# A graph layer's sums over edges on one core: four loads under way, 21 blocks of output kept back, and half as many paired sums

## The chip, the cores and the metric

The kernel runs on one NeuronCore of a Trainium2 chip. The metric is the device time of one execution in microseconds; three timed runs of the kernel before gave a median of 301.53 us (299.49 to 303.27). All data are float32.

## The reference

There are 12,500 nodes with 128 features and 412,500 edges with 48 features, sorted by their receiving node `dst`.

```
agg = segment_sum(edge_attr_48, dst, 12500)
h   = relu(layernorm(x))
u   = graph_globals[0]                       # every node belongs to graph 0
hid = relu(concat([h, agg, u]) @ W1 + b1)    # 256 wide
out = x + hid @ W2 + b2
```

The layer norm has no scale or shift of its own. The source nodes of the edges are not used.

## The kernel before, in words

**The sums over edges.** The edges are cut into 58 steps of 8 chunks; a chunk is 128 partitions by 7 edges. One load (`load`, line 297; the DMA itself is line 144) fetches two chunks, 336 KB, so a step has four loads; the last step has two, and a tail. For each step, VectorE builds a table of ones and zeros (`onehot`, line 308, tile `oh`) that says to which of 32 neighbouring nodes an edge goes. TensorE multiplies that table with the edges' features (`aggregate`, line 334) and adds up in PSUM (tile `ps`): eight chunks by seven places give 56 products of 32x48. ScalarE copies the result to `sums` (`keep_sums`, line 355), and about two steps later TensorE moves it to the right node rows with a second table (`place`, line 378, tile `pp`); VectorE adds it to the table of all sums `aggT` in SBUF (`add`, line 386).

The list `LEVELS` has one number for each step, 0 to 14. So many of the step's 14 groups (seven places, two halves of four chunks) are summed "by twos": two chunks are taken in one product of 64x96, of which only the two diagonal quarters are used. A group is then two products in place of four, and `keep_sums` makes two extra small copies in a step that has any.

```
if t >= n - twos:
    for q in range(0, CH, 2):
        c = CH * h + q
        product(ps[W * q:W * (q + 2), h], oh[:, c // 2, t], both[s][c // 2][:, :, t * DE:(t + 1) * DE],
                start=first, stop=end, skip_group_check=True)
    continue
```

**The layer.** The nodes are 26 blocks: one of 212 rows, 23 of 512, two of 256. For each block the rows of `x` are loaded (`load_x`, line 393), normalised (VectorE and ScalarE), turned (`turn`, tile `pt`), multiplied with the first weights (`first_h`, tile `ph`), and once all sums of the block are in, with the weights of the sums (`first_a`, tile `ph`); ScalarE takes the relu (`relu`, tile `hid`), TensorE the second product (`second`, tile `po`), VectorE adds x and b2 (`result`, line 527), and `store` (line 536) issues the output's DMA from POOL's queue (the last two blocks from SP's).

**The order.** It is written out by hand: each engine runs its instructions in the order in which the loop over steps (line 854) records them. The work of the layer is spread over half steps (`todo`, `at`) by a planner with a share of time for each. During step s the loads of step s + 3 are issued from SP's queue, one at each of four places in the step.

**What limits the loads.** `few` (line 290) makes each load wait until the load `FLIGHT` places before it has landed, and until TensorE has come to that place of the step (`last`):

```
def few(now):
    if len(flight) == FLIGHT:
        tc.add_manual_dep(now.ins, flight.pop(0).ins.name, LANDED, reason="few loads under way")
    flight.append(now)
    if paced:
        tc.add_manual_dep(now.ins, last[0], LANDED, reason="in TensorE's pace")
```

Loads of edges, of x and of node indices count alike. There are 18 buffers for loads of edges, four and a half steps' worth.

**Rows kept back.** The blocks in `HELD` do not get a buffer for their result: `result` writes it over the block's own, no longer needed columns of `aggT`, and `store` issues it in the last three steps (from half step 110 on, line 812), where few loads are left. The other blocks are stored as soon as they are done.

Of the kernel before, what the change touches and what calls it, by code (L numbers as in the profile page):

```python
# [22 lines left out]
def kernel(  # L23
# [38 lines left out]
    NS = NSF + 1  # L62
# [33 lines left out]
    NBL = len(blocks)  # L96
# [3 lines left out]

    FIRST = (1, 2, 3, 0, 4)

    HELD = range(NBL - 4 - 16, NBL - 4)
    ZN = 16
    zw = -(-(N + WG) // ZN)

# [43 lines left out]
    def rows_of(ap, a, m, r):  # L150
        return ap[a:a + m * r].rearrange("(p r) d -> p (r d)", r=r)
# [6 lines left out]
    with fast:  # L158
# [131 lines left out]
# [6 lines that stand above are left out]
# [38 lines left out]
        def aggregate(s, h, twos):  # L334
            left = s == NSF and h
            if h == 0:
                banks_s[s] = ps_agg.tile([P, 512], F32, name="ps")[:, :4 * DE].rearrange("p (h f) -> p h f", h=2)
            ps, es, oh = banks_s[s], edges[s], onehots[s]
            n = TT if left else T
            for t in range(n):  # L340
                first, end = t == 0 and h == 0, t == n - 1
# [6 lines that stand above are left out]
                for q in range(1 if left else CH):  # L348
                    c = CH * h + q
                    o = DE * (q % 2) if twos else 0  # L350
                    product(
                        ps[W * q:W * (q + 1), h, o:o + DE], oh[:, c // 2, t, c % 2], es[c][:, t * DE:(t + 1) * DE],
                        start=first, stop=end, skip_group_check=True)
# [32 lines left out]
        def add(s):  # L386
            _, v = nc.values_load_multi_w_load_instructions(  # L387
                at_i[0:1, s:s + 1], engines=[DVE], min_val=low(s), max_val=high(s),
                skip_runtime_bounds_check_because="clamped to these on the chip")
            to = aggT[:HI + DE, ds(v[0], WG)]  # L390
            nc.vector.tensor_tensor(to, to, banks_p.pop(s)[:HI + DE, :WG], OP.add)  # L391
# [135 lines left out]
        def result(j):  # L527
            a, m, r = blocks[j]
            if j in HELD:
                ot = aggT[:, BEFORE + a:BEFORE + a + r * D].rearrange("p (r d) -> p r d", d=D)  # L530
# [5 lines left out]
        def store(j):  # L536
# [3 lines left out]
            for p0, p1 in by_rows(m):  # L540
                now = queue.dma_start(rows_of(out, a + p0 * r, p1 - p0, r), ov[p0:p1])  # L541
                if j in HELD:
                    tc.add_manual_dep(now.ins, last[0], LANDED, reason="edges first")
# [58 lines left out]

        AHEAD = 4
        EARLY = 2
        FLIGHT = 5


        LEVELS = (0, 0, 0, 0, 7, 0, 0, 9, 14, 3, 14, 14, 0, 14, 3, 3, 2, 0, 5, 14, 0, 14, 2, 3, 0, 4, 14, 0, 14, 2, 4, 0, 3, 0, 5, 14, 0, 14, 0, 4, 0, 2, 0, 3, 14, 0, 14, 4, 2, 2, 0, 2, 2, 4, 0, 0, 0, 0)
        LATE = NS - 7
        NEAR = len(FIRST) + 1  # L610
        with tc.manual_schedule():
# [82 lines left out]
            def at(k, f, *a):  # L694
                todo.setdefault(max(0, k), []).append((f, a))
# [48 lines left out]
            for i in range(1, len(FIRST)):  # L744
                k = 2 * i
# [38 lines left out]
            for j in range(NW):  # L784
# [8 lines left out]
                if j + 1 < NW:  # L793
                    hidden_x(j + 1)
                    at(where["o", j] + 1, result, j)
                    if j not in HELD:
                        at(where["o", j] + 1, store, j)
# [3 lines left out]
            for j in range(NBL):  # L801
                if j in FIRST:
                    continue
                k = where["turn", j]
# [5 lines left out]
                at(k - 2, normal, j)  # L810
            at(where["a", 0] - 2, bias_of_globals)
            for i, j in enumerate(HELD):
                k = 2 * (NS - 3) + i // 3
                assert where["o", j] + 1 < k
                at(k, store, j)

# [3 lines left out]
            def apart(k, f, *a):  # L820
                while k - 1 in taken or k in taken or k + 1 in taken:
                    k -= 1
                taken.add(k)
                at(k, f, *a)
                return k
# [3 lines left out]
            for i in range(2, len(parts)):  # L829
                need = 2 * (parts[i][0] // CS - (4 if i == len(parts) - 1 else 0))  # L830
                k = apart(need - 4, middles, i)
                at(k + 2, check_dst, i)
                k = apart(k - 1, spread_dst, i, 1)
                k = apart(k - 1, spread_dst, i, 0)
# [5 lines left out]
            k = apart(2 * (NS - 6), verdict)  # L840
# [13 lines left out]
            for s in range(NS):  # L854
# [27 lines left out]
                if s >= LATE:  # L882
                    for p in now:
                        place(p)
                        add(p)
                twos = [max(0, LEVELS[s] - T), min(T, LEVELS[s])]
                aggregate(s, 0, twos[0])
# [175 lines left out]
```

## Time and profile before

| | |
|---|---|
| median of three timed runs | 301.53 us (299.49 to 303.27) |
| profiled execution | 298.43 us, of which the span is 296.6 us |
| TensorE (PE) busy | 283.1 us, 95% of the span |
| VectorE (DVE) busy | 237.0 us, 80% |
| ScalarE (ACT) busy | 161.0 us, 54% |
| POOL busy | 73.7 us, 25% |
| moved by DMA | 95.19 MB, mean 321 GB/s |
| loads of edges | 230 of 336 KB, median 5.2 us from issue to landing |
| mean granted TensorE clock | 0.991 |

PE is the matmul part of TensorE and PEld its weight loads, which overlap it. In the trace each float32 product shows as two records, so 56 products are "x112". In a row of the waits, the figures are the sum in microseconds, how often, and the longest. In a row of DMA issues they are how many, the size of each, and the median from issue to landing. In a row of the timeline they are the start, the length, the engine, the line, the operation, what it writes and reads, and how many were merged. In a row by windows each engine has its busy time and, in brackets, how many instructions ended there; the last three figures are the granted clock, the DMA engines' share of busy time and the rate.

### The profile page before, as it was taken

The page shows a single profiled execution, that of the slowest core. Times are in us where ns is not written, and L with a number is a line of the kernel's source. Part 1 is how long each engine was busy: PE and PEld are TensorE (multiplying, and loading weights), DVE is VectorE, ACT ScalarE, POOL GpSimd, SP SyncE. Part 2 cuts the span into 40 slices and gives each one's busy share as a digit, 9 for nine tenths or more (in the row PEclk, how much of TensorE's full clock was granted, in tenths as well). Part 3 has the DMA queues.
Part 4 walks back from the last instruction along what each step waited for, and adds up shares of the span by engine and source line. Part 5 has one row for each costly group of instructions (what it writes and reads, how often), then busy time and mean ns, then how long its engine had stood idle before and what let it go on. Part 6 is the DMA issues. An engine that isn't in the chain of part 4 may idle for free.

```text
span 296.6 us, 15062 instructions
## 1 busy us (share of the span) xinstructions
PE 283.1 (95%) x6553; PEld 223.5 (75%) x6554; DVE 237.0 (80%) x537; ACT 161.0 (54%) x399; POOL 73.7 (25%) x88
## 2 busy tenths in 40 slices
PE   6799897999999999999999999999999999999992
PEld 2657666898878778878878788867877977787781
DVE  6838969699998997887978699698986799986222
ACT  3477557323756664743666458644651985664420
POOL 3032381130212563021022212021111022103720
PEclk9999998999999999999999999999999999999998
DMA  6999999999999999999999999999999999999962
GB/s 162 372 314 345 272 358 313 370 370 370 356 357 356 326 367 285 298 348 290 332 312 339 346 345 317 336 321 322 310 347 337 353 298 323 337 352 317 363 222 81
DMA packets 69815, 95.19 MB, mean 321 GB/s; under 512 B 5018, under 2 KB 64739, under 8 KB 69743
## 3 DMA queue, kind: packets, MB, share of 16 engines
q1 hardware_dynamic: 67583, 87.66, 89.1%
q0 software_dynamic: 2160, 6.50, 6.1%
q8 instruction: 53, 0.87, 1.2%
q14 instruction: 19, 0.16, 0.1%
HBM read 87.74 MB, written 6.40 MB: 317 GB/s over the span
## 4 chain that ended last, share of the span: by engine, by line
PE 81%; DVE 8%; ACT 3%; DMA 2%; issue 2%; SPq 1%; DVEq 1%
PE ps L195 30%; PE ph L195 21%; PE po L195 14%; PE pp L195 10%; PE pt L199 5%; DVE oh L312 3%; DMA e<-in_edge_attr_dram 2%; DVE place L374 2%; ACT xn L438 1%; ACT hT L452 1%; PE pt L195 1%; DVE st L408 1%; DVE aggT L391 1%; DVE ph L489 1%; DVEq L387 1%
## 5 line engine op out<-in xcount | busy, mean ns | idle before, releaser
L312 DVE TENSOR_TENSOR oh<-iota,rel 128x1792 f32<-128x1792 f32 (+1 forms) x60 | 120.5, 2009 | 0.4 <-ACT rel L270 0.4
L195 PEld LDWEIGHTS ps<-e,oh 128*32 128x32 f32 (+1 forms) x5448 | 94.7, 116 | 21.7 <-issue 5.8
L195 PE MATMUL ps<-e,oh 128*32 128x48 f32 (+1 forms) x5448 | 106.5, 217 | 3.1 <-issue 1.2
L360 ACT COPY sums<-ps 128x192 f32<-128x192 f32 (+2 forms) x129 | 36.7, 285 | 78.7 <-PE ps L195 76.8
L431 POOL TENSOR_TENSOR xb<-xt,b_sb 128x512 f32<-128x512 f32 (+1 forms) x21 | 34.2, 1630 | 131.7 <-DVE aggT L533 79.4
L195 PE MATMUL ph<-hT,w1h 128*128 128x512 f32 (+2 forms) x100 | 49.6, 602 | 0.1
L195 PE MATMUL po<-w,hid 128*128 128x128 f32 (+1 forms) x376 | 48.0, 281 | 0.9 <-ACT hid L516 0.9
L516 ACT ACTIVATE hid<-ph,bias 128x512 f32<-128x512 f32 (+2 forms) x49 | 30.4, 670 | 30.4 <-PE ph L195 22.9
L195 PEld LDWEIGHTS po<-w,hid 128*128 128x128 f32 (+1 forms) x376 | 45.1, 196 | 2.0 <-ACT hid L516 1.3
L391 DVE TENSOR_TENSOR aggT<-aggT,pp 112x246 f32 x58 | 23.6, 406 | 24.5 <-PE pp L195 18.2
L195 PE MATMUL pp<-place,sums 128*112 128x128 f32 x232 | 39.0, 291 | 0.2 <-DVE place L374 0.2
L195 PEld LDWEIGHTS pp<-place,sums 128*112 128x112 f32 x232 | 28.9, 176 | 7.1 <-issue 1.7
L438 ACT ACTIVATE xn<-xt,sh,sc 128x128 f32<-128x128 f32 x80 | 33.1, 483 | 0.3
L374 DVE TENSOR_TENSOR place<-iota,pos 128x256 f32<-128x256 f32 x58 | 32.9, 569 | 0.0
L195 PE MATMUL ph<-aggT,w1a 48*128 48x256 f32 (+1 forms) x192 | 28.6, 402 | 0.2 <-DVE aggT L391 0.2
L195 PEld LDWEIGHTS ph<-aggT,w1a 48*128 48x128 f32 x192 | 17.2, 186 | 10.1 <-issue 6.8
L452 ACT COPY hT<-pt 128x512 f32<-128x512 f32 (+1 forms) x22 | 23.0, 1044 | 3.2 <-PE pt L199 3.1
L195 PEld LDWEIGHTS ph<-hT,w1h 128*128 128x128 f32 x100 | 16.7, 196 | 7.1 <-issue 4.6
L533 DVE TENSOR_TENSOR aggT<-po,xb 128x512 f32<-128x512 f32 x16 | 11.0, 685 | 9.2 <-PE po L195 9.2
L541 POOL DMA_DIRECT2D out_dram<-ot x9 | 5.0, 553 | 51.6 <-DVE ot L533 43.7
L408 DVE BATCH_NORM_STATS2 st<-xt 128x6 f32<-128x128 f32 x80 | 17.3, 277 | 0.0
L199 PE MATMUL pt<-ident,xn 128*128 128x128 f32 x84 | 14.1, 289 | 0.0
(137 smaller groups left out, 188.1 us busy)
## 6 DMA issues: line engine op xcount, KB each, us to landing
e<-in_edge_attr_dram SPq DMA_DIRECT2D x230, 336.0 KB, 5.2
xt<-in_x_dram SPq DMA_DIRECT2D x19, 256.0 KB, 4.9
out_dram<-aggT POOLq DMA_DIRECT2D x16, 256.0 KB, 4.5
out_dram<-ot POOLq DMA_DIRECT2D x7, 256.0 KB, 4.8
di<-in_dst_dram SPq DMA_DIRECT2D x3, 448.0 KB, 5.3
aggT<-in_x_dram SPq DMA_DIRECT2D x4, 256.0 KB, 4.2
xt<-in_x_dram SPq DMA_DIRECT2D x2, 128.0 KB, 4.6
out_dram<-ot SPq DMA_DIRECT2D x2, 128.0 KB, 3.3
```

What stands on the lines that cost most here:

```text
L195: last[:] = [nc.tensor.matmul(*a, **k).ins.name]
L199: last[:] = [nc.tensor.transpose(*a, **k).ins.name]
L312: nc.vector.tensor_tensor(to, iota[:, None, :W].to_broadcast([P, n, W]), r[:, :, None].to_broadcast([P, n, W]), OP.is_equal)
L360: nc.scalar.copy(to[k, h], ps[k, h, None, o:o + DE].to_broadcast([k.stop - k.start, h.stop - h.start, 2, DE]))
L374: nc.vector.tensor_tensor(po, iota[:, None, :WP].to_broadcast([P, 2, WP]), pos[:, s, :, None].to_broadcast([P, 2, WP]), OP.is_equal)
L391: nc.vector.tensor_tensor(to, to, banks_p.pop(s)[:HI + DE, :WG], OP.add)
L408: nc.vector.bn_stats(st[:m, q, :], xs[j][:m, q, :])
L431: nc.gpsimd.tensor_tensor(xb[:m, :r], xs[j][:m, :r], b2_sb[:m, None, :].to_broadcast([m, r, D]), OP.add)
L438: nc.scalar.activation(xn[:m, q], xs[j][:m, q], AF.Relu, bias=shift[j][:m, q:q + 1], scale=scale[j][:m, q:q + 1])
L452: nc.scalar.copy(hT[:, :m * r].rearrange("d (p r) -> d r p", r=r), ht[j][:, :m * r].rearrange("d (r p) -> d r p", r=r))
L516: nc.scalar.activation(to, ph, AF.Relu, bias=bias[:, h:h + 1])
L533: nc.vector.tensor_tensor(ot[:m, :r], pos_o[j][:m, :r], xbs[j][:m, :r], OP.add)
```

## The change

`FLIGHT` goes from 5 to 4: a load waits for the one four places before it. `HELD` takes blocks 1 to 21 in place of 6 to 21, so 21 results are kept in `aggT` and stored in the last three steps, four to a half step in place of three. `LEVELS` is another list: its sum is 121 in place of 248, and 29 of its entries are not zero in place of 35. Up to step 29 the sums are 63 and 155, up to step 50 they are 115 and 240.

```diff
-    HELD = range(NBL - 4 - 16, NBL - 4)
+    HELD = range(1, NBL - 4)
...
-        FLIGHT = 5
+        FLIGHT = 4
...
-        LEVELS = (0, 0, 0, 0, 7, 0, 0, 9, 14, 3, 14, 14, 0, 14, 3, 3, 2, 0, 5, 14, 0, 14, 2, 3, 0, 4, 14, 0, 14, 2, 4, 0, 3, 0, 5, 14, 0, 14, 0, 4, 0, 2, 0, 3, 14, 0, 14, 4, 2, 2, 0, 2, 2, 4, 0, 0, 0, 0)
+        LEVELS = (0, 0, 0, 0, 8, 3, 2, 0, 3, 14, 0, 14, 2, 1, 0, 3, 0, 1, 2, 0, 0, 2, 0, 2, 0, 1, 0, 2, 0, 3, 0, 0, 5, 0, 14, 0, 14, 4, 0, 3, 0, 2, 1, 0, 2, 0, 2, 1, 0, 4, 0, 0, 3, 0, 3, 0, 0, 0)
...
             for i, j in enumerate(HELD):
-                k = 2 * (NS - 3) + i // 3
+                k = 2 * (NS - 3) + i // 4
                 assert where["o", j] + 1 < k
                 at(k, store, j)
```

## The prediction

> **What bounds the kernel now.** I read the page first, from its span and busy shares to the chain of waits.
>
> ```profile
> span 296.6 us, 15062 instructions
> PE 283.1 (95%) x6553; PEld 223.5 (75%) x6554; DVE 237.0 (80%) x537; ACT 161.0 (54%) x399; POOL 73.7 (25%) x88
> ...
> PE 81%; DVE 8%; ACT 3%; DMA 2%; issue 2%; SPq 1%; DVEq 1%
> ```
>
> TensorE is busy in 95% of the span and carries 81% of the chain. That looks like a plain TensorE bound, so I asked by stretch of time, for all engines and the DMA.
>
> ```profile
> core 0: us, PE busy (x) PEld busy (x) DVE busy (x) ACT busy (x) POOL busy (x), PEclk, DMA share, GB/s
> 60.00:110.00 50.00, 49.84 (x1140) 40.87 (x1138) 48.14 (x103) 27.32 (x70) 15.91 (x16) 1.00 1.05 358
> 110.00:160.00 50.00, 50.00 (x1203) 40.68 (x1202) 40.34 (x90) 28.58 (x68) 9.17 (x8) 1.00 0.97 314
> 160.00:210.00 50.00, 50.00 (x1263) 39.11 (x1262) 42.18 (x86) 27.55 (x68) 10.01 (x8) 1.00 1.00 330
> 210.00:271.00 61.00, 61.00 (x1518) 48.40 (x1518) 52.76 (x128) 36.61 (x97) 10.13 (x8) 1.00 1.00 332
> ```
>
> From 60 to 271 us two things are full at once: TensorE never pauses, and the DMA engines are busy 0.97 to 1.05 of the time. Which of them leads? The waits of SP's queue, which issues the loads, answer it.
>
> ```profile
> SPq L144 <- DMA e<-in_edge_attr_dram: 108.2, 176, 2.4
> ...
> SPq L144 <- PE pp L195: 6.5, 15, 1.1
> ```
>
> SP waits 108 us for an earlier load to land (the limit of five under way) and only a few us at a time for TensorE's pace. So the loads come as fast as that limit lets them. The next question is how early they are when TensorE needs them. Step 30's last load is the 124th and step 51's the 208th; I looked up when they were issued and when those steps' sums began. A landing is counted from the start of the issue.
>
> ```profile
> 150.48 0.37 SPq L144 DMA_DIRECT2D e<-in_edge_attr_dram  x1
> e<-in_edge_attr_dram SPq DMA_DIRECT2D x124, 336.0 KB, 5.3
> 155.76 1.87 PE L195 MATMUL ps<-e,oh 128*32 128x48 f32 x96
> ...
> 247.79 0.37 SPq L144 DMA_DIRECT2D e<-in_edge_attr_dram  x1
> e<-in_edge_attr_dram SPq DMA_DIRECT2D x208, 336.0 KB, 5.2
> DMA to landing us min/median/max: 5.2/5.2/5.2
> 253.73 1.71 PE L195 MATMUL ps<-e,oh 128*32 128x48 f32 x104
> ```
>
> Both singly took 5.2 us. Load 124 lands at 150.5 + 5.2 = 155.7; it is needed in the second half of step 30's sums, at about 155.8 + 0.7 = 156.4: 0.7 us to spare. Load 208 lands at 253.0 and is needed at 253.7 + 0.7 = 254.4: 1.4 us to spare. So TensorE's long work and the loads run side by side, and a shorter TensorE meets the loads at once.
>
> **The change part by part.** *The list.* One unit of it makes two products of 64x96 out of four of 32x48. A step with none and a step with 14 show its price:
>
> ```profile
> 212.22 1.40 PE L195 MATMUL ps<-e,oh 128*32 128x48 f32 x112
> 213.55 0.69 PE L195 MATMUL pp<-place,sums 128*112 128x128 f32 x4
> ...
> 146.57 2.53 PE L195 MATMUL ps<-e,oh 128*64 128x96 f32 x56
> 149.03 0.69 PE L195 MATMUL pp<-place,sums 128*112 128x128 f32 x4
> ```
>
> From the first product to the next group it is 213.55 - 212.22 = 1.33 us with none and 149.03 - 146.57 = 2.46 us with 14, so a unit costs 1.13 / 14 = 0.081 us: the paired form is the slower one. The list falls from 248 to 121 units; 127 x 0.081 = 10.3 us leave TensorE. Of these, 92 units (7.5 us) stand before step 30 and 125 (10.1 us) before step 51. With fewer steps that pair (29 in place of 35), ScalarE makes 12 fewer extra copies of sums, of 230 to 310 ns each:
>
> ```profile
> L360 ACT COPY sums<-ps 32x96 f32<-32x96 f32 x45 | 10.3, 230 | 1.0
> L360 ACT COPY sums<-ps 32x192 f32<-32x192 f32 x26 | 8.1, 310 | 0.6
> ```
>
> That is 3 us off an engine that is 54% busy: nothing, since its other work covers it, and if that cover were gone it would only gain.
>
> *The output rows.* Blocks 1 to 5 are no longer stored between 50 and 105 us; all 21 go out in the last three steps, four to a half step. Five stores of 256 KB at the 358 GB/s of the stretch in which they ran are 5 x 262,144 B / 358 GB/s = 3.7 us of DMA time. Bounds for the loads: 3.7 us earlier, if the engines' bytes are the limit (their share there was 1.05), or nothing, if only the loads under way are (358 GB/s fell to 314 to 332 once the stores had stopped, so the loads did not speed up by themselves). I take 3.7, because a DMA share of 1.05 leaves no idle engine that could carry a store for nothing. At the end, POOL issues 5 more, 0.54 us each:
>
> ```profile
> 272.16 3.21 POOL L541 DMA_DIRECT2D out_dram<-aggT  x6 [3.48 <-PE pt L199]
> 276.46 1.60 POOL L541 DMA_DIRECT2D out_dram<-aggT  x3 [1.09 <-PE pt L199]
> ...
> 281.26 2.13 POOL L541 DMA_DIRECT2D out_dram<-aggT  x4 [1.09 <-PE ph L195]
> 290.40 0.54 POOL L541 DMA_DIRECT2D out_dram<-ot  x1 [7.01 <-DVE ot L533]
> ```
>
> The first burst grows from 6 to 8 (4.3 us, until 276.4, when the next may start anyway), the last from 4 to 5. POOL sat idle 7.0 us before its last store, more than 5 x 0.54 = 2.7 us, and behind it nothing waits. The DMA engines have room as well: the last two of the 40 slices (7.4 us each) moved 222 and 81 GB/s.
>
> ```profile
> GB/s 162 372 314 345 272 358 313 370 370 370 356 357 356 326 367 285 298 348 290 332 312 339 346 345 317 336 321 322 310 347 337 353 298 323 337 352 317 363 222 81
> ```
>
> I cost this end at 0; with that room gone it would be the 3.7 us again. VectorE writes these blocks' results into the table of sums in place of a buffer, in the same time, and POOL's queue loses five waits for results in mid run, which only lets the sums with b2 behind them start sooner.
>
> *Four loads under way.* A load's turn is its landing time over the loads under way:
>
> ```profile
> e<-in_edge_attr_dram SPq DMA_DIRECT2D x230, 336.0 KB, 5.2
> DMA to landing us min/median/max: 4.1/5.2/6.8
> ```
>
> Now it is 5.2 / 5 = 1.04 us. With four it depends on how far the landing shortens. The lower bound is the shortest landing seen, 4.1: 4.1 / 4 = 1.025, by step 51 a gain of 0.015 x 208 loads = 3.1 us. An upper bound is that the landing only loses the carriage of the one load less, 344,064 B / 358 GB/s = 0.96 us: (5.2 - 0.96) / 4 = 1.06, a loss of 0.02 x 208 = 4.2 us. Farther off, a landing that stays at 5.2 would give 1.30, or 54 us; the queue in front of a load cannot stay as long with one load less in it, so what lies beyond 1.06 is left to a rival. I take the middle of the two near ends, a loss of 0.5 us. The waits stand in SP's queue, and behind a waiting load stand only more loads, x rows and indices; TensorE waits for them.
>
> The Trainium skill, "DMA: Bandwidth & Descriptors", Anatomy of one DMA, puts a DMA at about 2.0 us fixed plus its bytes at 436 GB/s. For 336 KB that is an estimate of 2.8 us, and four under way would then cost nothing: the sum would be 0.5 us better. No row here shows a load alone; the shortest landing of 4.1 us lies well above it.
>
> *The sum.* TensorE can be earlier only as far as the loads are. At step 51: 1.4 (to spare) + 3.7 (stores) - 0.5 (turn) = 4.6 us, less than the 10.1 us taken out by then. At step 30: 0.7 + 3.7 - 0.3 (124 loads) = 4.1, against 7.5 us. After step 51 only 2 units more go, and the loads regain their lead. So 4.6 of 10.3 us are kept and about 5.7 us come back as waits for loads. The profiled execution took 298.43 us (span 296.6 and 1.8 around it): 298.43 - 4.6 = 293.8, or 0.9846 of it. The median of the runs shown, 301.53, is 1.0% above that execution; times 0.9846 it is 296.9 us. The bounds give 298.43 - (1.4 + 3.7 + 3.1) = 290.2 and 298.43 - (1.4 + 0 - 4.2) = 301.2, as medians 293.2 and 304.4.
>
> **The rivals.** *The loads keep up.* With fewer under way the landing may shorten more than in proportion; then all 10.3 us are kept: 288.1, as a median 291.1. For it: the loads stretched to 0.97 to 1.05 DMA share while moving 314 to 358 GB/s, so some of their time is not carriage. Against it: step 51's last load would have to come 8.7 us earlier, and the stores and the best turn give 3.7 + 3.1 = 6.8.
>
> *Four are too few.* If the landing falls only to 4.4 us, the turn is 1.10 us, 0.06 x 208 = 12.5 us later at step 51: +12.5 - 5.1 = 7.4, 305.8, as a median 309.0. It beats a 2% loss from 6.0 + 5.1 = 11.1 us on, a turn of 1.093 and a landing of 4.37. For it: from 160 us on no load landed in under 4.3 us.
>
> ```profile
> DMA to landing us min/median/max: 4.3/5.2/5.9
> DMA to landing us min/median/max: 4.3/5.1/5.4
> ```
>
> (These are 160 to 210 and 210 to 271 us.) Against it: those had four others in front of them. A starved TensorE also loses its clock:
>
> ```profile
> 45.50:49.00 3.50, 1.91 (x69) 1.54 (x57) 3.50 (x7) 1.86 (x6) 0.23 (x1) 1.00 0.97 319
> 49.00:52.50 3.50, 3.50 (x51) 3.27 (x53) 3.50 (x4) 2.57 (x8) 0.84 (x2) 0.52 0.93 290
> ```
>
> After a stretch with 1.91 of 3.5 us busy, it ran the next 3.4 us at about half clock, some 1.7 us lost. In my forecast the 5.7 us of waits lie over more than 30 steps, 0.2 us each, so I count none; where loads come in clumps, each clump costs 1.7 us more. The Trainium skill, "TensorE: Matmul & The Clock Gate", Part 1, has the clock halved after a whole idle window of about 3.4 us; by that rule no wait here would do it. The trace is stricter: half a window idle was enough.
>
> *All of it comes back.* If the stores free nothing and the turn costs the 1.4 us to spare, the list's 10.3 us turn into waits and the time stays at 301.5. For it: the loads' rate did not rise when the stores stopped.
>
> VectorE as the next bound (48.1 of 50 us busy from 60 to 110) would hold back early steps alone; from 110 on it has 14% or more to spare, and the loads bind there.
>
> **How the numbers follow.** Forecast 0.48, its own range 293 to 304: some 0.17 of it under 295.5, 0.07 over 307.6 through clumped waits, 0.24 between. The loads keep up 0.21 (faster). Four too few 0.23 (slower). All comes back 0.08 (same). That is 0.38 faster by over 2%, 0.32 within 2% (about what a measurement of this kernel can tell from no change), 0.30 slower. The range of 289 to 309 takes in the rivals' times and leaves out about 2 in 10.
>
> **What would show it.** Right: the 32x48 products rise by 508 and the 64x96 ones fall by 254 in the program, TensorE's busy time falls by about 10 us, and waits of its sums for the loads appear between steps 20 and 51, 4 to 8 us in all; the median landing falls to about 4.2 us; SP's waits for landings grow; no store between 55 and 260 us, and the last held store is issued about 7 us before the last store of all, as now. Wrong: a landing above 4.4 us, TensorE still without waits (the loads kept up), a granted clock under 0.98, or an end that waits for stores.

## The result, and the profile after

| | before | after |
|---|---|---|
| median of the timed runs | 301.23 us (299.49 to 303.27) | 330.76 us (327.59 to 334.1) |
| ratio | | 1.094, interval 1.083 to 1.106: slower |
| profiled execution | 298.43 us | 327.59 us |
| mean granted TensorE clock | 0.991 | 0.964 |

Executions of one kernel differ by 1 to 3%, some of them longer at a lower granted clock; the ratios in this document compare only the quicker ones.

The page of the changed kernel: its span, TensorE's row, and the chain of waits by engine.

```profile
span 325.8 us, 16060 instructions
...
PE 288.3 (88%) x7061; PEld 223.9 (69%) x7062; DVE 231.7 (71%) x537; ACT 156.5 (48%) x387; POOL 83.4 (26%) x88
...
DMA 55%; PE 40%; issue 2%; SPq 2%; ACT 0%; DVE 0%; DVEq 0%
```

The chain was 81% TensorE and 2% DMA; now more than half of it is waiting for transfers. The same middle stretch by windows, first of before, then of after (columns as in the prediction):

```profile
80.00:225.00 145.00, 145.00 (x3483) 115.83 (x3483) 123.03 (x267) 82.93 (x202) 32.72 (x29) 1.00 1.00 330
```

```profile
80.00:225.00 145.00, 132.31 (x3417) 103.85 (x3409) 106.28 (x236) 70.32 (x170) 36.72 (x23) 0.96 0.93 296
```

TensorE, never idle in this stretch before, lacks 12.7 of 145 us, and the transfers have become slower (330 to 296 GB/s), not faster. Who waits for whom: SP's queue in the changed kernel, then the sums' weight loads and products in it, then the products before.

```profile
SPq L144 <- DMA e<-in_edge_attr_dram: 132.3, 188, 2.1
```

```profile
PEld ps L195 <- DMA e<-in_edge_attr_dram: 28.4, 35, 2.3
...
PE ps L195 <- DMA e<-in_edge_attr_dram: 23.0, 31, 2.2
```

```profile
PE ps L195 <- DMA e<-in_edge_attr_dram: 0.9, 2, 0.5
```

SP's wait for earlier loads grew from 108 to 132 us, and the sums' products now wait 23 us for loads (0.9 before; the weight loads' row is largely the same idle time seen on the other half of TensorE, and is not added to it). The loads themselves, in the view of line 144 (shortest, median and longest issue in ns; first and last start), of before and of after:

```profile
L144 SPq DMA_DIRECT2D e<-in_edge_attr_dram x230: 367/368/1955, 2.6 to 270.8; - x115
```

```profile
L144 SPq DMA_DIRECT2D e<-in_edge_attr_dram x230: 367/368/1512, 2.6 to 299.2; - x115
...
DMA to landing us min/median/max: 3.6/4.7/7.7
```

The last load is issued 299.2 - 270.8 = 28.4 us later: nearly the whole 29 us. The landing fell from 5.2 only to 4.7 us, so the turn rose from 5.2 / 5 = 1.04 to 4.7 / 4 = 1.175 us; 0.135 x 208 = 28 us by step 51. The issue records of the two traces bear it out: load 208 is issued at 274.3 us, 26.5 us later than before. The end is as before: eight stores in the first burst, a last store on POOL with idle time ahead of it.

```profile
296.49 4.32 POOL L541 DMA_DIRECT2D out_dram<-aggT  x8 [3.94 <-PE pt L199]
...
312.89 0.54 POOL L541 DMA_DIRECT2D out_dram<-aggT  x1 [0.35 <-PE pp L195]
319.16 0.54 POOL L541 DMA_DIRECT2D out_dram<-ot  x1 [5.73 <-DVE ot L533]
```

### The profile page after: what moved, and what is told of

Its sections match the earlier page's. It is cut to its first block, busy times and chain, and to the rows that moved or that the text cites. A ratio compares the mean times of both kernels' runs of the same rounds, so it can differ in the third digit from the quotient of the medians.

```text
span 325.8 us, 16060 instructions
## 1 busy us (share of the span) xinstructions
PE 288.3 (88%) x7061; PEld 223.9 (69%) x7062; DVE 231.7 (71%) x537; ACT 156.5 (48%) x387; POOL 83.4 (26%) x88
## 4 chain that ended last, share of the span: by engine, by line
DMA 55%; PE 40%; issue 2%; SPq 2%; ACT 0%; DVE 0%; DVEq 0%
DMA e<-in_edge_attr_dram 51%; PE ps L195 16%; PE ph L195 9%; PE po L195 8%; PE pp L195 5%; DMA aggT<-in_x_dram 3%; PE pt L199 2%; DMA xt<-in_x_dram 1%; SPq L144 1%; PE pt L195 0%; SPq L580 0%; SPq L398 0%; ACT sums L360 0%; ACT hid L516 0%; DVE ot L533 0%
## 5 line engine op out<-in xcount | busy, mean ns | idle before, releaser
L195 PE MATMUL ps<-e,oh 128*32 128x48 f32 (+1 forms) x5956 | 109.5, 216 | 25.8 <-DMA e<-in_edge_attr_dram 23.0
L195 PEld LDWEIGHTS ps<-e,oh 128*32 128x32 f32 (+1 forms) x5956 | 92.4, 115 | 49.6 <-DMA e<-in_edge_attr_dram 28.4
L312 DVE TENSOR_TENSOR oh<-iota,rel 128x1792 f32<-128x1792 f32 (+1 forms) x60 | 118.0, 1968 | 0.4 <-ACT rel L270 0.4
L431 POOL TENSOR_TENSOR xb<-xt,b_sb 128x512 f32<-128x512 f32 (+1 forms) x21 | 44.0, 2094 | 186.5 <-DMA xt<-in_x_dram 107.2
L360 ACT COPY sums<-ps 128x192 f32<-128x192 f32 (+2 forms) x117 | 32.7, 281 | 110.0 <-PE ps L195 108.5
L195 PE MATMUL ph<-hT,w1h 128*128 128x512 f32 (+2 forms) x100 | 47.8, 583 | 0.5 <-ACT hT L452 0.5
L195 PE MATMUL pp<-place,sums 128*112 128x128 f32 x232 | 41.2, 303 | 1.0 <-DVE place L374 1.0
L195 PEld LDWEIGHTS pp<-place,sums 128*112 128x112 f32 x232 | 30.7, 186 | 8.1 <-issue 2.4
L374 DVE TENSOR_TENSOR place<-iota,pos 128x256 f32<-128x256 f32 x58 | 28.6, 494 | 0.0
L541 POOL DMA_DIRECT2D out_dram<-aggT x21 | 11.3, 543 | 8.4 <-PE pt L199 3.9
```

What stands on the lines that cost most here:

```text
L195: last[:] = [nc.tensor.matmul(*a, **k).ins.name]
L312: nc.vector.tensor_tensor(to, iota[:, None, :W].to_broadcast([P, n, W]), r[:, :, None].to_broadcast([P, n, W]), OP.is_equal)
L360: nc.scalar.copy(to[k, h], ps[k, h, None, o:o + DE].to_broadcast([k.stop - k.start, h.stop - h.start, 2, DE]))
L374: nc.vector.tensor_tensor(po, iota[:, None, :WP].to_broadcast([P, 2, WP]), pos[:, s, :, None].to_broadcast([P, 2, WP]), OP.is_equal)
L431: nc.gpsimd.tensor_tensor(xb[:m, :r], xs[j][:m, :r], b2_sb[:m, None, :].to_broadcast([m, r, D]), OP.add)
```

## The experiments

### The three parts, one at a time

**Four loads under way alone (e1).**

```diff
-        FLIGHT = 5
+        FLIGHT = 4
```

> FLIGHT 4 alone; the list of sums by twos and the rows kept are those of before. Theory A (the turn of a load): with four under way the landing stays near 4.7 us, the turn near 1.18 us, and 208 loads come 0.135 x 208 = 28 us later; so 325 to 331 us, SP's waits for landings above 125 us, whatever the list. Rival B (the list: with fewer sums by twos TensorE empties its buffers in clumps, waits, and runs at half clock): with the old list the loads are not asked for so early, TensorE hides most of the slower turn, 303 to 312 us. Rival C (the stores, 5 more at the end): 301 us here.

Measured: 329.89 us, ratio 1.088 (1.078 to 1.099). This part makes the whole loss, with the old list too, so the list's fill does not hide it. The products wait as in the changed kernel:

```profile
PE ps L195 <- DMA e<-in_edge_attr_dram: 27.0, 33, 2.7
```

**The rows kept alone (e2, and once more as e16).**

```diff
-    HELD = range(NBL - 4 - 16, NBL - 4)
+    HELD = range(1, NBL - 4)
...
-                k = 2 * (NS - 3) + i // 3
+                k = 2 * (NS - 3) + i // 4
```

> 21 blocks' rows kept to the last three steps, five loads under way, the old list. Theory A: the stores are no part of the loss, 299 to 302 us; if the five stores' bytes (3.7 us) had been in the loads' way, the time to spare of the loads grows but TensorE's work is the same, so no gain shows. Rival C (the end waits for 21 stores): 305 to 310 us, with the last two slices full of stores.

> The rows kept alone, again, to learn whether its 0.9% is real: 0.985 to 0.997 of before if so (the loads have time to spare, the stores leave the full stretch, and the end has room for them); 0.998 to 1.002 if it was chance.

Measured: 299.65 us, ratio 0.991 (0.986 to 0.996), and again 298.63 us, 0.994 (0.990 to 0.998). A small gain of about 2 us, just clear of the noise in both; the end does not pay for it. Where the 2 us come from was not shown. It is the one part worth keeping, and this kernel beats both.

**The half list alone (e3), and with the rows kept (e4).** The diff is the line `LEVELS` of the change; e4 has the two edits of e2 as well, so it is the changed kernel with five loads under way.

> The list with 121 units alone, five loads under way, 16 blocks kept. Theory A: TensorE has 10.3 us less work, but a load's turn stays 1.04 us and only 1.4 us are to spare at step 51, so 298 to 301 us, with 6 to 9 us of new waits of the sums for loads. Rival B (missing fill brings clumps at half clock): 305 to 315 us, granted clock under 0.98.

> The changed kernel with FLIGHT 5 in place of 4. Theory A: the whole loss goes, and what the prediction said without its term for four under way should show: 301.2 - 1.4 - 3.7 = 296 us, or 299 if the stores free nothing. Rival B or C: most of the loss stays, 315 to 330 us.

Measured: 309.1 us, ratio 1.024 (1.015 to 1.032); and 308.31 us, 1.025 (1.015 to 1.034). Theory A is wrong here: TensorE has less work, the loads are limited as before, and the kernel is 7 us slower. The time is one that rival B gives, but not its cause: the granted clock is 0.987, not under 0.98. The waits of e3:

```profile
PE ps L195 <- issue: 8.0, 11, 2.0
...
PE ps L195 <- DMA e<-in_edge_attr_dram: 1.0, 2, 0.5
```

The products of the sums wait 8 us for something that the profile names "issue", its word for nothing it can show, and 1 us for loads; between 50 and 280 us all products together wait 14.4 us in this way, and none do before. So the loads are in time, and something else is late. The timeline shows where: TensorE stops in the midst of a row of equal products. Four stretches of e3, each from just before the end of one such stop to just before the end of the next, by windows:

```profile
139.59:144.74 5.15, 4.57 (x127) 2.86 (x127) 5.12 (x12) 2.31 (x6) 0.75 (x1) 1.00 1.05 364
144.74:149.69 4.95, 4.44 (x127) 4.10 (x127) 3.62 (x16) 2.89 (x7) 0.00 (x0) 1.00 0.99 332
149.69:154.84 5.15, 4.68 (x126) 3.33 (x127) 5.12 (x5) 2.54 (x7) 2.63 (x1) 1.00 0.99 307
154.84:159.77 4.93, 4.35 (x128) 3.35 (x127) 2.30 (x5) 2.23 (x7) 1.85 (x2) 1.00 1.01 349
```

Each holds 253 to 255 records of TensorE (about 127 of products and 127 of weight loads), whatever they were, in 4.9 to 5.2 us. And the DMA queues have one that carries instructions, in before and in e3:

```profile
q8 instruction: 53, 0.87, 1.2%
```

```profile
q8 instruction: 57, 0.93, 1.3%
```

0.87 MB in 53 packets is 16.4 KB each; e3 has 4 packets more for 1016 more records of TensorE (508 products and 508 weight loads), 254 to a packet. So the new theory: TensorE waits for its own code, which comes in packets of some 256 instructions, one about every 5 us while the loads run. The packet records of the traces, read one by one, bear it out. Between 50 and 280 us TensorE stops, products and weight loads both, 20 times for over 0.3 us in e3, and each of the 20 stops ends 1.2 to 1.6 us after a packet of instructions has landed; they make 16.4 us. Before has no such stop there. A unit of the list replaces four products by two: it costs 0.08 us of work but saves 8 instructions, a 32nd part of a packet, 8 / 256 x 5 = 0.16 us where code is what TensorE waits for. The Trainium skill, "Runtime: NRT & Kernel Launch", Instruction fetch mechanics, has code come in blocks of 16 KiB, 256 instructions; the trace agrees with 16.4 KB. The same section calls the cost of a boundary mostly hidden; here it is not, with 7 us.

### Is it the code?

**Six loads under way: with the old list (e5), with the half list (e6).** Both have the rows kept and `FLIGHT = 6`.

> Before's list, 21 blocks kept, FLIGHT 6. Theory L (only the loads under way count): the turn falls from 1.04 us to about 1.0 (landing about 6 us, the engines being full), TensorE's work is that of before, so 297 to 300 us. Theory C (TensorE also waits for its own code: packets of 16 KB on the queue marked instruction, 53 of them, which come behind the loads): each packet waits for one load more, and new waits marked issue show; 301 to 308 us.

> The changed kernel with FLIGHT 6. Theory L: no slower than with five under way, 300 to 308 us. Theory C: with the half list TensorE runs through 256 instructions faster than the next packet of code comes; with six under way the packet comes later still, so slower than the 308 us with five: 312 to 330 us, the waits marked issue up from 13 us to over 25 us on the sums' weight loads.

Measured: e5 301.39 us, ratio 1.004 (0.999 to 1.010); e6 312.21 us, 1.037 (1.028 to 1.046). A sixth load brings nothing: in e5 SP's wait for landings falls to 43 us, from 108 in before, and it waits for TensorE's pace instead, so the loads were early enough with five. The time lies at the foot of theory C's range, but the sums' products wait only 2.7 us marked issue, so it says little for C.

```profile
SPq L144 <- DMA e<-in_edge_attr_dram: 43.2, 88, 1.4
SPq L144 <- PE ps L195: 25.0, 25, 2.0
```

e6 lies above e4, as the theory of the code has it, but the intervals overlap and the sums' weight loads wait 15.1 us marked issue (e4: 12.9), not the 25 expected. That one load more delays the code is not shown by this pair.

**No sums by twos (e7).**

```diff
-        LEVELS = (0, 0, 0, 0, 7, 0, 0, 9, ...
+        LEVELS = (0,) * 58
```

> No sums by twos at all (248 units less than before, 20 us less of TensorE's work), 21 blocks kept, FLIGHT 5. Theory L, and the prediction's reckoning by TensorE's work: 296 to 308 us, no worse than the half list. Theory C: 248 x 8 = 1984 more instructions than before, 7.75 more packets of code, at 5.05 us a packet where TensorE waits for each: about 60 x 5.05 + 8 = 311, so 310 to 320 us, with a step between waits of just 256 instructions.

Measured: 321.22 us, ratio 1.063 (1.051 to 1.074), just above theory C's range, where by TensorE's work alone it should have been the fastest. Its waits, three rows of its timeline in which the stops stand in brackets, and the two stretches between these stops by windows:

```profile
PE ps L195 <- issue: 31.3, 32, 2.3
...
PE ps L195 <- DMA e<-in_edge_attr_dram: 1.4, 3, 0.5
```

```profile
75.66 0.63 PE L195 MATMUL ps<-e,oh 128*32 128x48 f32 x39 [0.93 <-issue]
...
80.69 0.63 PE L195 MATMUL ps<-e,oh 128*32 128x48 f32 x40 [1.12 <-issue]
...
86.59 0.72 PE L195 MATMUL ps<-e,oh 128*32 128x48 f32 x48 [1.61 <-issue]
```

```profile
75.56:80.59 5.03, 3.91 (x127) 3.10 (x127) 4.97 (x13) 3.12 (x8) 0.00 (x0) 1.00 1.02 343
80.59:86.50 5.91, 4.29 (x128) 3.97 (x127) 5.88 (x17) 2.25 (x4) 2.79 (x4) 1.00 1.00 321
```

It waits 31 us without a cause that the profile can name, and loads cost it 1.4. The stops move through the step (39, 40 and 48 records of products before the end of its sums), and from one to the next there are 254 and 255 records, in 5.03 and in 5.91 us: they follow the count of instructions, not the work. Between 50 and 280 us e7 has 29 stops of over 0.3 us, 29.9 us in all, and each of them ends 1.2 to 1.6 us after a packet of instructions has landed.

**The same without most loads (e9), and before's list without most loads (e10).** Both have the rows kept and five loads under way. After step 7 no edges are loaded; the later steps sum the buffers of steps 4 to 7 again. That leaves out 198 of the 230 loads (the text below says 182); the tail is summed as before.

```diff
-                    edges[s].append(etail)
+                    edges[s] = edges[s][:4] + [etail]
                 return
+            if s >= 8:
+                edges[s], both[s] = edges[s % 4 + 4], both[s % 4 + 4]
+                return
             for c in (2 * i,):
```

> No sums by twos, rows kept, FLIGHT 5, but no edges are loaded after the first eight steps: later steps sum the buffers of steps 4 to 7 again. Left out: 182 of the 230 loads of edges. Theory C1 (the packets of code come late because they stand behind the loads): without loads the waits at every 256th instruction vanish, and TensorE's 20 us less work than before shows in full: 275 to 282 us. Theory C2 (a packet of code takes some 5 us whatever else runs): the waits stay, 305 to 322 us as with the loads.

> The same with before's list: the loads of edges stop after eight steps. Both theories: TensorE's own work sets the end, 293 to 298 us. Compared with the kernel without pairs it shows what a unit of the list costs when neither loads nor code are in the way: 20 us for 248 units if the prediction's 0.081 us holds.

Measured: 283.68 and 289.42 us for e9, 294.88 and 298.24 us for e10. Without the loads the order turns round: no pairs is 11 us faster than before's list by the quicker run of each, where with the loads it was 22 us slower (e7 against e2). The middle stretch of e7, then of e9:

```profile
80.00:225.00 145.00, 125.62 (x3705) 97.70 (x3705) 110.55 (x240) 65.68 (x147) 26.62 (x22) 1.00 0.96 309
...
PE ps L195 <- issue: 15.9, 16, 1.6
```

```profile
80.00:225.00 145.00, 144.73 (x4439) 113.88 (x4440) 131.05 (x296) 78.87 (x189) 35.22 (x22) 1.00 0.13 37
...
PE ps L195 <- issue: 0.2, 1, 0.2
```

Same list, same instructions: with 309 GB/s of loads beside it TensorE waits 15.9 us for code in this stretch, with 37 GB/s it waits 0.2 and gets through 734 more records of products. So the loads make the code late (C1), and a packet does not take 5 us whatever else runs (C2). The packet's own transfer takes as long with the loads as without (a median of 1.05 and 1.04 us in this stretch), so the time is lost ahead of it; where, is not shown. Not all of the waits go with the loads: e9 came out 2 to 7 us above the expected range, and 8.6 us of waits of this kind stayed in the whole of it, nearly all outside this stretch. Three of them come after the last load, which was issued at 40.3 us:

```profile
PE ps L195 <- issue: 3.0, 3, 1.4
```

```profile
61.38 0.62 PE L195 MATMUL ps<-e,oh 128*32 128x48 f32 x36 [1.36 <-issue]
...
65.60 0.55 PE L195 MATMUL ps<-e,oh 128*32 128x48 f32 x32 [0.93 <-issue]
```

The first line is of 46 to 80 us; from 54 to 66 us all transfers together made 26 GB/s. Each of the three ends 1.4 to 1.5 us after a packet has landed, and the last two end 4.2 us apart, with one packet between them. So code can be late without the loads as well, where TensorE gets through a packet in less than about 4 us (an estimate from these two stops); from 80 to 225 us one lasted it 4.15 us on average. TensorE's busy time in e10 and e9 prices the list:

```profile
PE 280.9 (96%) x6553; PEld 222.2 (76%) x6554; DVE 233.6 (80%) x537; ACT 160.9 (55%) x399; POOL 76.4 (26%) x88
```

```profile
PE 259.2 (92%) x7545; PEld 202.0 (72%) x7546; DVE 234.5 (83%) x537; ACT 139.6 (50%) x329; POOL 83.6 (30%) x88
```

21.7 us for 248 units, 0.087 us each.

**Four loads with before's list and the rows kept (e15)**: the changed kernel with before's `LEVELS`.

> The changed kernel with before's list: rows kept, FLIGHT 4. With the loads 28 us late the list has no say: 326 to 331 us, TensorE's waits for loads shorter by the 10 us that it works more. If the list's code packets still cost something with four loads under way, it is quicker than the changed kernel by some us: 320 to 325.

Measured: 329.04 us, ratio 1.099 (1.088 to 1.109), the same as the changed kernel's 1.094 (1.083 to 1.106). With four loads under way the list has no say in the time, neither for its work nor for its code: between 50 and 280 us the changed kernel's TensorE stops 24 times for over 0.3 us, and only 2 of the stops end 1.2 to 1.6 us after a packet of code. So the list's 7 us and FLIGHT's 28 are not to be added.

### Why the landing hardly shortens

**One load alone (e8)**: the changed kernel with `FLIGHT = 1`.

> The changed kernel with FLIGHT 1, one look for the landing of a load with no other load beside it. If landing is in proportion to the loads under way (1.04 to 1.18 us each), it is 1.1 us; if it has a part that does not shrink, by the line through 4.7 us (four) and 5.2 us (five) it is 4.7 - 3 x 0.5 = 3.2 us, and the time is about 255 x 3.2 + 20 = 840 us. The Trainium skill, DMA: Bandwidth & Descriptors, Anatomy of one DMA, gives an estimate of 2.8 us for 336 KB (2.0 us fixed and the bytes at 436 GB/s).

Measured: 852.45 us in a single run, and

```profile
e<-in_edge_attr_dram SPq DMA_DIRECT2D x230, 336.0 KB, 3.0
```

Both are near what the line through the two points gave (840 us, 3.2 us). A load with no other beside it lands in 3.0 us, with three others in 4.7, with four others in 5.2: each further load adds 1.7 / 3 = 0.57 and then 0.5 us, about half of the 0.96 us that its bytes take at the rate of the full stretch. In proportion to the number it would have been 4.2 us with four. The estimate of 2.8 us from the Trainium skill, "DMA: Bandwidth & Descriptors", Anatomy of one DMA, is close to the 3.0 for a load alone, though that section measures DMAs issued by GpSimd and these are issued by SP; that four would cost nothing, which the prediction drew from it, does not hold.

**Halved loads, eight and ten under way (e11, e12).** Both have before's list and the rows kept.

```diff
-                few(load_edges(e, s * CS + c, 2))
+                few(load_edges(e, s * CS + c, 1))
+                few(load_edges(e[:, 1:], s * CS + c + 1, 1))
```

> Before's list, rows kept, each load of 336 KB cut into two of 168 KB, and eight of them under way: the bytes under way of FLIGHT 4. Theory S (four loads do not fill 16 engines because a place comes free only when the slowest engine has ended its share; smaller loads come free sooner): turn per 336 KB 1.05 to 1.1 us, 300 to 315 us. Theory F (a fixed part of some 2 us in every landing, in which its place carries nothing): the same share of bytes idles, turn about 1.18 us, 325 to 331 us as with FLIGHT 4.

> As the one before, with ten loads of 168 KB under way: the bytes of FLIGHT 5. Theory S: the engines are full already, so no quicker than five loads of 336 KB: 298 to 301 us. Theory C: as many bytes stand before a packet of code as before, so no new waits; with 230 more issues of 0.37 us SP's queue has 0.74 us per 336 KB, under the turn of 1.04.

Measured: 327.91 us, ratio 1.083 (1.067 to 1.099), and 326.56 us, 1.082 (1.069 to 1.094). The same, with eight and with ten, so the number under way does not decide any more. In e11:

```profile
L144 SPq DMA_DIRECT2D e<-in_edge_attr_dram x460: 327/430/2096, 2.6 to 299.3; - x154
```

```profile
SPq L144 <- DMA e<-in_edge_attr_dram: 10.4, 25, 0.9
```

```profile
149.65 7.77 SPq L144 DMA_DIRECT2D e<-in_edge_attr_dram  x13
```

SP hardly waits for landings (10 us, from 139 in e1): 460 issues in 297 us are 0.65 us apart. The median issue takes 0.43 us, but some take much longer: the mean is 0.50 us, 231 us for all 460, and in the last line 13 of them with no wait between fill 7.77 us, 0.60 us each. So SP's queue had become the bound, which expectation C of e12 had ruled out by reckoning 0.37 us each; why some issues take longer is not shown. On the landing the pair says nothing.

**Doubled loads, two and three under way (e13, e14).** One load of four chunks (672 KB), nine buffers in place of 18, rows kept, before's list.

```diff
-        ep = fast.enter_context(tc.tile_pool(name="edges", bufs=18))
+        ep = fast.enter_context(tc.tile_pool(name="edges", bufs=9))
...
-            for c in (2 * i,):
-                e = ep.tile([P, 2, T * DE], F32, name="e")
-                few(load_edges(e, s * CS + c, 2))
-                edges.setdefault(s, []).extend([e[:, 0], e[:, 1]])
-                both.setdefault(s, []).append(e)
+            if i % 2:
+                return
+            e = ep.tile([P, 4, T * DE], F32, name="e")
+            few(load_edges(e, s * CS + 2 * i, 4))
+            edges.setdefault(s, []).extend([e[:, c] for c in range(4)])
+            both.setdefault(s, []).extend([e[:, 0:2], e[:, 2:4]])
```

> Before's list, rows kept, loads of 672 KB (four chunks), two under way: the bytes of four loads of 336 KB, with half as many issues. Theory B (what counts is the bytes under way): the turn per 336 KB stays 1.18 us, 325 to 331 us. Theory S (a place is idle from when its fast engines have ended until the slowest has): coarser places lose more, 345 to 375 us.

> The same with three loads of 672 KB under way, the bytes of six. Theory B: as with FLIGHT 6, 299 to 303 us. Theory S: between four and five loads of 336 KB, 305 to 320 us.

Measured: 393.32 us (384.16 to 397.03), and 316.04 us, ratio 1.050 (1.040 to 1.059): the first above the ranges of B and of S, the second within that of S. The landings, of e13 and of e14:

```profile
e<-in_edge_attr_dram SPq DMA_DIRECT2D x115, 672.0 KB, 5.3
```

```profile
e<-in_edge_attr_dram SPq DMA_DIRECT2D x115, 672.0 KB, 6.1
```

Two of 672 KB take turns of 5.3 / 2 = 2.65 us, 1.33 per 336 KB, where four of 336 KB with as many bytes had 1.175. So the bytes under way are not all that counts: fewer, larger places lose more, as S says. Three give 6.1 / 3 = 2.03, 1.02 per 336 KB, as good as five of 336 KB. Both kernels are slower than these turns say. Each of the loads of x rows and indices (256 KB and the like) also takes up one of only two or three places, and in e13 the issues of x rows wait 47 us for loads of edges (11 before), so their times are not a clean measure. That S's own mechanism (the slowest engine's share holds the place) is the cause was not shown.

## Why the prediction was wrong

**The step that failed is the turn with four under way.** The prediction took 1.025 to 1.06 us as the bounds and 0.5 us as the cost; it is 1.175 us and 28 us. The mechanism stood there (landing over loads under way, and the rival "Four are too few"), and the term was mis-sized. The upper bound was the error: "the landing only loses the carriage of the one load less" was meant as the worst case, but it supposes that every load in front costs its full 0.96 us. It costs half of that (e8), since a load alone spends 3.0 us, most of it not as carriage at the full rate. The excluded far end, a landing that stays at 5.2 (54 us), was no farther from the truth than the middle that was taken; the reason given for leaving it out, that a queue with one load less must be shorter, bounds the direction and not the size. The rival named its point rightly (a landing over 4.37 us loses) but priced the case at 4.4, at its own edge, and the range ended there, at 309.

**The list: the price was right, the conclusion was wrong.** 0.081 us a unit (0.087 in e10 against e9), 10.3 us out of TensorE. What was to keep part of it from being gained, late loads, is not what happened with five loads under way: e3's sums wait 1 us for loads, and it is 7 us slower, through code. The page of before had the queue with 53 packets of instructions; the prediction put an added instruction at nothing, without a reason. In the changed kernel it does not decide, by e15.

**The rows kept: right within its bounds.** 3.7 us taken, 0 to 3.7 given; e2 and e16 show about 2 us with the old list; with the half list nothing is to be seen (e4 against e3). The end at 0 held: POOL idles 5.7 us before its last store.

**Clumps at half clock: counted none, and there are some.** The granted clock fell from 0.991 to 0.964. In the changed kernel's trace TensorE ran at half clock in six stretches of 3.4 us (before: one) and once at the end, and in the 3.4 us ahead of each of the six it was busy, products and weight loads taken together, for 1.0 to 2.5 us. At the prediction's 1.7 us each, the five that are new make 8.5 us, most of what the list had taken out. One of them, the 3.4 us ahead of it and then its own:

```profile
124.90:128.31 3.41, 1.54 (x80) 0.94 (x82) 1.53 (x1) 0.98 (x4) 3.34 (x2) 1.00 0.94 289
128.31:131.72 3.41, 3.41 (x62) 2.87 (x52) 1.16 (x5) 0.32 (x1) 0.00 (x0) 0.50 1.05 329
```

But the clock is 0.985 in e1 and 0.966 in e15, whose times are the same, so this belongs to the loss and does not set it: the loads' last issue at 299 us sets it.

**What was to be seen.** The counts of products, SP's longer waits and the stores' end came as written. The waits of the sums for loads came, but 23 us of them in place of 4 to 8. TensorE's busy time did not fall by 10 us; it rose from 283.1 to 288.3. Beside e15, the same kernel with before's list, it is 10.0 us lower (298.3): the list's work did go, and the waiting and the slower clock put more back. Of the signs of being wrong, the landing above 4.4 us and the clock under 0.98 showed.

## What to carry to other kernels

When a limit of transfers under way is lowered, do not take the carriage off the landing: the turn is landing over number, the landing of one alone is its floor, and between the two known points a line is the safer guess; a limit that just fills the engines has all of its loss right below it. Before work is taken out of an engine by replacing few large instructions with many small ones, divide its instructions by the packets of its code and ask whether the next packet comes in time beside the other transfers. A wait marked issue that returns after a fixed count of instructions, in the midst of equal work, is that wait.

## What the runs showed of the hardware that was not expected

- TensorE's code comes in packets of 16.4 KB, some 256 instructions. Beside 307 to 364 GB/s of transfers one came about every 5 us where TensorE waited for it (4.9 to 5.2 us in the four stretches of e3). With 37 GB/s there was no wait to speak of from 80 to 225 us (0.2 us against 15.9), though with 26 GB/s, from 54 to 66 us, TensorE still waited twice, 2.3 us in all.
- A stop for code ended 1.2 to 1.6 us after the packet had landed, in all 49 stops of over 0.3 us that e3 and e7 have between 50 and 280 us.
- TensorE's clock was halved for 3.4 us after 3.4 us in which it was busy for 1.0 to 2.5 us, six times in the changed kernel: a wholly idle stretch was not needed.
- Landing of 336 KB: 3.0 us alone, 4.7 with four, 5.2 with five under way; so five move 330 GB/s and four 296 in the same stretch.
- Issues of 168 KB loads stood 0.65 us apart in a queue that waited only 10 us for landings; the median issue took 0.43 us and the mean 0.50.
